# Column blocks for the projections of four fused attention layers on one Trainium2 core

## The chip, the cores and the metric

The kernel runs on one core of one Trainium2 chip, alone. A core has TensorE for matmuls (the profile splits it into PE, the matmuls, and PEld, the loads of their stationary operand), VectorE (DVE), ScalarE (ACT), GpSimd (POOL) and SyncE (SP, here the engine whose queue issues most of the transfers). Matmuls write to PSUM, and VectorE and ScalarE carry their results from there to SBUF. The metric is the device time of one execution in microseconds; the median of some runs is compared.

## The reference, cut to what matters

Four residual layers follow each other on an image batch x of shape (4, 56, 56, 256), all in fp32. Each layer first normalises x over 32 groups of channels (`_gn`).

```
x = x + _L0_conv_ref(_gn(x), ...)   # 7x7 neighbourhood attention, zero padding
x = x + _L1_conv_ref(_gn(x), ...)   # dense graph of 1024 tokens per block
x = x + _L2_conv_ref(_gn(x), ...)   # 7x7 neighbourhood attention, dilation 1 and 2
x = x + _L3_conv_ref(_gn(x), ...)   # 7x7 shifted window attention
return x
```

Layers 0, 2 and 3 share one frame; here it is with the names of layer 2:

```
qkv = (x @ w_qkv + b_qkv).reshape(B, H, W, 3, NUM_HEADS, hd)
...
attn = jnp.einsum('bhijd,bhijkld->bhijkl', q, kg)
attn = attn + rpb[...]
...
attn = jax.nn.softmax(attn.reshape(B, h, H, W, ks * ks), axis=-1)
...
return jnp.einsum('bhijkl,bhijkld->bhijd', attn, vg)
...
return out @ w_proj + b_proj
```

There are 8 heads of 32 channels. A layer thus has four projections of 256 by 256 for each token: queries, keys, values and the output.

## The kernel before

The program's main part is `direct_blocks`; a second, slower form (`fused_blocks`) stands behind a test of the input's range and isn't run here. An image has 3,136 tokens. Channels lie on partitions in two halves (CC = 2), so x is held as 128 partitions by 2 by tokens, and a projection adds up two matmuls, h = 0 and 1, of 128 contracted channels each.

**Projections.** `project` (L941 to L947) makes 128 output channels for 392 tokens (layers 2 and 3, and the output projection of layer 0) or 448 tokens (keys and queries of layer 0): the stationary operand is a 128 by 128 piece of the weight, the normalised tokens stream past it, and the result takes one PSUM bank of tag m, of which there are two (`ps_m`). It is called for keys, queries and the output projection. `value_tiles` (L962 to L980) makes the values the other way round: 128 tokens are stationary and the 256 columns of the weight stream, so that tokens come to lie on partitions; two such tiles share a bank. The last tile of an image has 64 tokens (the 25th). VectorE adds the bias (L975), and the values go to HBM, from where the attention gathers them.

**Attention.** It goes in units. In layers 0 and 2 (`attend_pairs`) a unit is a tile of 7 rows and 12 or 16 columns, for all heads or for four heads of two tiles; in layer 3 (`attend_quads`) it is four heads of eight windows. The logits (L1058, L1012) contract over the 32 channels of one head: four heads are stationary on four blocks of 32 rows of the array at once. VectorE, ScalarE and GpSimd add the masks, take the exponential and multiply by a mask or bias (L1065 to L1069, L1017 to L1019); GpSimd adds two pieces into b (L1078). The products (L1087, L1027) give 32 output channels for each head: four heads write to four blocks of 32 columns, which are the PSUM partitions `j * HD:(j + 1) * HD`. A second set of them, with ones for the values, gives the denominators. VectorE divides (L1237, L1841, L2075, and L1239, L1845, L2077).

**Order.** The work of a unit is written out as logits of this unit, then `fill`, then products of the unit before it:

```
for w in units:
    logits(w)
    if held:
        both(held)
    w["fill"]()
    if held:
        products(held)
        held["done"]()
    held = w
```

`fill` holds the steps of the other work, dealt out over the units by `stream` in each layer: the projections for rows that are needed later (`project_rows`), the values (`values`), the output projection of earlier rows (`project_out`), normalising (`prepare`), and one step of the group statistics (`step_stats`). The statistics have two small matmuls of full width for each layer and image (L912, L921). TensorE so goes from logits in row blocks to projections of the full 128 by 128 array, and from these to products in column blocks, once in nearly every unit. There are 128 units in each of layers 0 and 2 and 64 in layer 3. A scheduler orders layers 0 and 2; layer 3 follows the written order on TensorE, VectorE, ScalarE and GpSimd. Layer 1 uses neither `project` nor `value_tiles`. All four engines wait for each other through semaphores.

The code that the change touches, and what calls it:

Of the kernel before, what the change touches and what calls it, by code (L numbers as in the profile page):

```python
# [34 lines left out]
C = 256  # L35
P = 128
CC = C // P
HD = 32
# [792 lines left out]
def direct_blocks(ctx: ExitStack, tc: tile.TileContext, d: dict, watch):  # L831
# [3 lines left out]
    nc = tc.nc  # L835
# [40 lines left out]
    def ps_m():  # L876
        return psum_tile("m", m_bufs)
# [63 lines left out]
    def project(w, col, rhs, n):  # L941

        pm = ps_m()
        for h in range(CC):
            nc.tensor.matmul(pm[:, :n], lhsT=w[:, h, col:col + P], rhs=rhs(h),  # L945
                             start=(h == 0), stop=(h == CC - 1))
        return pm[:, :n]  # L947

    def evac(i, dst, src):
# [12 lines left out]
    def value_tiles(v, a, c, n, xn, w, bias, dst):  # L962

        t0, t1 = c * n // P, (c + 1) * n // P if (c + 1) * n < T else -(-T // P)
        pm = ps_m()
        sizes = [min(P, T - t * P) for t in range(t0, t1)]
        mine = sizes[2 * a:2 * a + 2]
        for j, k in enumerate(mine):
            first = (2 * a + j) * P
            for h in range(CC):  # L970
                nc.tensor.matmul(pm[:k, j * C:(j + 1) * C], lhsT=xn[:, h, first:first + k], rhs=w[:, h, :],  # L971
                                 start=(h == 0), stop=(h == CC - 1))
        for k in sorted(set(mine)):
            js = [j for j, kj in enumerate(mine) if kj == k]
            nc.vector.tensor_tensor(  # L975
                v[:k, 2 * a + js[0]:2 * a + js[-1] + 1, :], pm[:k, js[0] * C:(js[-1] + 1) * C].rearrange("p (j c) -> p j c", c=C),
                bias[:k].rearrange("p (o c) -> p o c", o=1).to_broadcast([k, len(js), C]), ALU.add)
            t = t0 + 2 * a + js[0]
            nc.sync.dma_start(out=dst[t * P:min((t + len(js)) * P, T), :].rearrange("(k p) c -> p k c", p=k),
                              in_=v[:k, 2 * a + js[0]:2 * a + js[-1] + 1, :])  # L980
# [145 lines left out]
    def layer0(early, big, pool, brief):  # L1126
# [47 lines left out]
        def project_rows(r):  # L1174
# [6 lines left out]
            def values(a):  # L1181
                value_tiles(v, a, g, CH, xn, wv, bv0, vd[b])

            def keys(m):
                pm = project(wk, m * P, lambda h: xn[:, h, at:at + CH], CH)
                rows = pm.rearrange("p (r c) -> p r c", c=S)
                for i in range(NTC):
                    c0, n = key_range(*COLS[i:i + 2])
                    dst = (kE if i in (0, NTC - 1) else kI)[:, m, i // 2, 8 * g:8 * (g + 1), :]
                    nc.scalar.activation(dst, rows[:, :, c0:c0 + n], AF.Identity, bias=bk0[:, m:m + 1])  # L1190

            def queries(m):
                pm = project(wq, m * P, lambda h: xn[:, h, at:at + CH], CH)
                y = 8 * g
                while y < 8 * (g + 1):
                    i, y1 = y // TR, min((y // TR + 1) * TR, 8 * (g + 1))
                    if (b, i) not in q:
                        q[b, i] = brief.tile([P, CC, BT], FP, tag="q", name="q0", bufs=6)
                    nc.scalar.activation(q[b, i][:, m, (y - TR * i) * S:(y1 - TR * i) * S],
                                         pm[:, (y - 8 * g) * S:(y1 - 8 * g) * S],  # L1200
                                         AF.Identity, bias=qbias[:, 0, m:m + 1], scale=SCALE)
                    y = y1
# [53 lines left out]
        def project_out(r):  # L1256
            b, g = divmod(r, NB0)
            x = pool.tile([P, CC, BT], FP, tag="xr", name="xr0")
            nc.sync.dma_start(out=x, in_=tokens_of(0, b, g * BT, BT))

            def step(m):
                pm = project(wo, m * P, lambda h: attns[r][:, h, :], BT)
                nc.vector.scalar_tensor_tensor(x[:, m, :], pm, bo0[:, m:m + 1], x[:, m, :], ALU.add, ALU.add)
                if m:
                    add_stats(1, b, g, x)
                    nc.sync.dma_start(out=tokens_of(1, b, g * BT, BT), in_=x)
            return [lambda m=m: step(m) for m in range(CC)]
# [465 lines left out]
    def layer2(held, big, pool, brief, last_steps):  # L1733
# [27 lines left out]
        def project_rows(i):  # L1761
# [9 lines left out]
            def values(a):  # L1771
                value_tiles(v, a, c, WC2, xn, w_qkv[:, :, 2 * C:], bv2, vd[b])
# [206 lines left out]
    def layer3(early, big, pool, brief):  # L1979
# [69 lines left out]
        def values(r):  # L2049

            b, c = divmod(r, 8)
            xn = xns[r]
            v = pool.tile([P, 4, C], FP, tag="vt", name="vt3", bufs=1)

            def step(a):
                value_tiles(v, a, c, WC, xn, w_qkv[:, :, 2 * C:], bv3, vd[b])
                if a == 0 and r:
                    gather(r - 1)
                if a and r == NIMG * 8 - 1:
                    gather(r)  # L2060
            return [lambda a=a: step(a) for a in range(2)]
# [195 lines left out]
```

## Time and profile before

| | us |
|---|---|
| median of 3 runs | 3989.01 |
| lowest and highest run | 3976.07, 3992.41 |
| span of the profiled execution | 3977.8 |
| TensorE matmul busy | 3814.5 (96%) |
| VectorE busy | 2372.2 (60%) |
| GpSimd busy | 1745.8 (44%) |
| ScalarE busy | 1381.2 (35%) |

The span runs from the first to the last instruction of the profiled execution. Mean granted TensorE clock is 0.983 of full speed. A matmul's end in the trace is modelled and matmuls overlap, so busy time says little of how near TensorE is to its peak; the starts are what counts. An fp32 matmul of the program appears as two matmuls and two weight loads in the trace, called passes below. In a shape such as `128*32 128x392` the first pair is rows and columns of the array in use, the second the partitions and columns of the streamed operand. The lines that carry the argument stand in the prediction.

### The profile page before, as it was taken

How to read it: one execution, taken by the hardware profiler on the slowest of the kernel's cores; microseconds unless marked ns; L12 is line 12 of the kernel's file. 1: busy time of each engine (PE TensorE's matmuls, PEld its weight loads, DVE VectorE, ACT ScalarE, POOL GpSimd, SP SyncE). 2: the span in 40 equal slices, each digit the busy share in tenths (PEclk: the TensorE clock that was granted, in tenths of full speed). 3: DMA queues.
4: the chain of work that ended last, by engine and by line, in shares of the span. 5: the costliest groups of instructions: out<-in, count | busy, mean ns of one | idle time of the engine just before them, and what ended most of it. 6: DMA issues, size and time to landing. Idle time of an engine off the chain costs nothing. (4 is left out here: it accounts for less than half of the span.)

```text
span 3977.8 us, 92350 instructions
## 1 busy us (share of the span) xinstructions
PE 3814.5 (96%) x38871; PEld 2707.4 (68%) x38871; DVE 2372.2 (60%) x4431; ACT 1381.2 (35%) x2927; POOL 1745.8 (44%) x1883
## 2 busy tenths in 40 slices
PE   7999999889999999999999999999999999899998
PEld 4566666557777677776777767776676666566765
DVE  6777777734345544445444553446788887666665
ACT  3455545422222222222222222222555555344443
POOL 3566767721123312233112331123677777555554
PEclk9899999989999999999999999999999999999999
DMA  8343333320000100001000000001344443434442
GB/s 270 104 134 119 113 120 104 99 104 1 24 19 24 40 6 15 20 25 35 6 24 15 25 24 10 10 10 56 111 125 126 125 121 111 157 120 135 127 128 93
DMA packets 268659, 301.84 MB, mean 76 GB/s; under 512 B 25926, under 2 KB 260584, under 8 KB 267752
## 3 DMA queue, kind: packets, MB, share of 16 engines
q1 hardware_dynamic: 267946, 295.76, 23.9%
q8 instruction: 308, 5.05, 0.5%
q14 instruction: 117, 0.96, 0.1%
q10 hardware_dynamic: 288, 0.08, 0.0%
HBM read 203.39 MB, written 92.37 MB: 74 GB/s over the span
## 5 line engine op out<-in xcount | busy, mean ns | idle before, releaser
L1441 DVE TENSOR_TENSOR acc<-acc,ps_v 128x257 f32<-128x257 f32 x1104 | 463.4, 423 | 718.7 <-PE ps_v L1519 690.7
L1519 PE MATMUL ps_v<-xw,e 128*128 128x257 f32 x2208 | 612.6, 382 | 1.2 <-DVE acc L1441 1.2
L1514 PE MATMUL ps_o<-xw,at 128*128 128x257 f32 x2208 | 609.0, 379 | 0.0
L1409 PE MATMUL ps_s<-xnT,xd 128*128 128x512 f32 (+3 forms) x1344 | 572.7, 549 | 3.9 <-DVE xnT L1387 3.9
L1519 PEld LDWEIGHTS ps_v<-xw,e 128*128 128x128 f32 x2208 | 413.5, 189 | 142.7 <-issue 82.4
L1503 ACT COPY at<-ps_t 128x512 f32<-128x512 f32 (+3 forms) x332 | 170.6, 514 | 970.0 <-PE ps_t L1500 969.7
L1078 POOL TENSOR_TENSOR b<-e 126x336 f32<-126x336 f32 (+5 forms) x512 | 500.0, 997 | 9.6 <-ACT e L1066 1.5
L1514 PEld LDWEIGHTS ps_o<-xw,at 128*128 128x128 f32 x2208 | 419.1, 190 | 60.1
L945 PE MATMUL ps_m<-xn,w_wqkv 128*128 128x392 f32 x1024 | 379.1, 504 | 12.3 <-DVE dv L922 3.9
L1402 POOL TENSOR_SCALAR xd<-xnT,vec 128x128 f32<-128x128 f32 x192 | 116.8, 619 | 569.3 <-PE ps_s L1409 565.7
L1069 POOL TENSOR_TENSOR e<-e,m0t 126x672 f32<-126x672 f32 (+3 forms) x128 | 238.6, 1864 | 265.8 <-ACT e L1068 245.4
L1069 POOL TENSOR_TENSOR e<-e,bias 119x784 f32<-119x784 f32 (+5 forms) x128 | 244.0, 1906 | 179.9 <-ACT e L1068 178.6
L1409 PEld LDWEIGHTS ps_s<-xnT,xd 128*128 128x128 f32 x1344 | 225.8, 191 | 141.8 <-issue 126.5
L1412 ACT ACTIVATE e<-ps_s 128x512 f32<-128x512 f32 x336 | 185.4, 552 | 347.8 <-PE ps_s L1409 340.8
L990 ACT ACTIVATE no<-rs 128x168 f32<-128x168 f32 (+2 forms) x256 | 93.8, 367 | 583.8 <-DVE rs L1841 268.3
L945 PEld LDWEIGHTS ps_m<-xn,w_wqkv 128*128 128x128 f32 x1024 | 187.8, 191 | 137.3 <-ACT pr L2097 17.5
L1087 PEld LDWEIGHTS ps_o<-e,vp 124*32 124x32 f32 (+3 forms) x8192 | 177.8, 111 | 147.4 <-issue 97.7
L1087 PE MATMUL ps_o<-e,vp 124*32 124x112 f32 (+3 forms) x8192 | 242.0, 254 | 6.2 <-POOL e L1069 4.4
L1841 DVE RECIPROCAL rs<-ps_o 128x196 f32<-128x196 f32 (+2 forms) x128 | 176.0, 1375 | 87.1 <-PE ps_o L1087 86.6
L939 DVE TENSOR_SCALAR xn<-x,gst 128x28 f32<-128x28 f32 (+4 forms) x368 | 207.5, 616 | 32.3 <-PE ps_m L945 22.9
L1066 ACT ACTIVATE e<-e 126x672 f32<-126x672 f32 (+5 forms) x256 | 219.5, 857 | 20.7 <-DVE e L1065 8.0
L1019 POOL TENSOR_TENSOR e<-e,m3l 98x784 f32<-98x784 f32 x64 | 118.3, 1848 | 217.9 <-ACT e L1016 217.9
(196 smaller groups left out, 6293.8 us busy)
## 6 DMA issues: line engine op xcount, KB each, us to landing
x<-xr SPq DMA_DIRECT2D x64, 392.0 KB
x<-in_x SPq DMA_DIRECT2D x53, 448.0 KB
x<-x SPq DMA_DIRECT2D x60, 392.0 KB
xr<-x SPq DMA_DIRECT2D x60, 392.0 KB
vd<-v SPq DMA_DIRECT2D x72, 256.0 KB
xr<-in_x SPq DMA_DIRECT2D x32, 392.0 KB
xr<-x SPq DMA_DIRECT2D x28, 448.0 KB
x<-xr SPq DMA_DIRECT2D x28, 448.0 KB
```

What stands on the lines that cost most here:

```text
L939: nc.vector.tensor_scalar(dst, src, gst[:, h, 0:1], gst[:, h, 1:2], ALU.subtract, ALU.mult)
L945: nc.tensor.matmul(pm[:, :n], lhsT=w[:, h, col:col + P], rhs=rhs(h), start=(h == 0), stop=(h == CC - 1))
L1066: nc.scalar.activation(ev, ev, AF.Exp)
L1069: nc.gpsimd.tensor_tensor(parts(ev), parts(ev), w["emask"], ALU.mult)
L1078: nc.gpsimd.tensor_tensor(w["b"][a][:nk, :, :2 * nq].rearrange("p h (i c) -> p h i c", i=2), ev[:, :, :, 0, :], ev[:, :, :, 1, :], ALU.add)
L1087: nc.tensor.matmul(w["o"](k, i)[j * HD:(j + 1) * HD], lhsT=ones[:nk, :HD] if k else v(j, u), rhs=w["b"][j // 2][:nk, j % 2, i * nq:(i + 1) ...
L1409: nc.tensor.matmul(s[:, :n], lhsT=xd[j][:, h, :], rhs=xnT[:, h, first * P:last * P], start=(h == 0), stop=(h == CC - 1))
L1412: nc.scalar.activation(e[:, :n], s[:, :n], AF.Exp, scale=5.0)
L1441: nc.vector.tensor_tensor(acc[:, i, :], acc[:, i, :], pv[:, :C + 1], ALU.add)
L1514: nc.tensor.matmul(out[j][:, :C + 1], lhsT=e[:, col(i)] if i == j else at[:, col(i)], rhs=xw[:, i, :], start=(i == j), stop=(i == NB - 1))
L1519: nc.tensor.matmul(pv[:, :C + 1], lhsT=e[:, col(i)], rhs=xw[:, j, :], start=True, stop=True)
L1841: nc.vector.reciprocal(rs.rearrange("p (t c) -> p t c", t=2), pv[:, :, 1, :])
```

## The change

In `project` each of the two matmuls becomes four, and each writes 32 of the 128 partitions of the same bank, from 32 columns of the weight piece, with the same streamed operand. In `value_tiles` the stationary tokens are cut in the same way, k / 32 blocks for a tile of k tokens (four, or two for the last tile of an image). Everything that reads the results is as it was.

```
         pm = ps_m()
         for h in range(CC):
-            nc.tensor.matmul(pm[:, :n], lhsT=w[:, h, col:col + P], rhs=rhs(h),
-                             start=(h == 0), stop=(h == CC - 1))
+            for j in range(4):
+                nc.tensor.matmul(pm[j * HD:(j + 1) * HD, :n], lhsT=w[:, h, col + j * HD:col + (j + 1) * HD], rhs=rhs(h),
+                                 start=(h == 0), stop=(h == CC - 1))
         return pm[:, :n]
...
             for h in range(CC):
-                nc.tensor.matmul(pm[:k, j * C:(j + 1) * C], lhsT=xn[:, h, first:first + k], rhs=w[:, h, :],
-                                 start=(h == 0), stop=(h == CC - 1))
+                for i in range(0, k, HD):
+                    nc.tensor.matmul(pm[i:i + HD, j * C:(j + 1) * C], lhsT=xn[:, h, first + i:first + i + HD], rhs=w[:, h, :],
+                                     start=(h == 0), stop=(h == CC - 1))
```

## The prediction

> **What bounds the kernel now.** I first cut the span into the layers (busy time by window), then asked what TensorE waits for, then read one unit of attention in the timeline. The windows are the start-up, layers 0, 1, 2 and 3; the columns after the length are busy microseconds and instruction counts by engine.
>
> ```profile
> 0.00:88.00 88.00, 60.42 (x546) 38.70 (x550) 56.45 (x121) 29.05 (x72) 24.68 (x27) 0.96 0.83 278
> 88.00:804.00 716.00, 651.57 (x10915) 435.85 (x10908) 541.30 (x764) 340.88 (x794) 476.90 (x378) 0.95 0.38 114
> 804.00:2757.00 1953.00, 1930.67 (x8668) 1419.08 (x8666) 887.41 (x2294) 426.34 (x790) 488.29 (x757) 0.99 0.07 23
> 2757.00:3443.00 686.00, 657.82 (x11435) 457.41 (x11435) 537.52 (x730) 362.25 (x861) 488.61 (x399) 0.99 0.42 125
> 3443.00:3978.00 535.00, 514.00 (x7318) 356.35 (x7318) 349.50 (x526) 222.72 (x411) 267.36 (x322) 0.98 0.39 121
> ```
>
> TensorE is busy 91, 96 and 96% in layers 0, 2 and 3; the next engine, VectorE, has 76, 78 and 65%. The waits of TensorE with a cause are few; these are its largest.
>
> ```profile
> PE ps_m L945 <- DVE attn L1239: 19.0, 10, 3.7
> PE ps_m L912 <- DVE mv L908: 14.2, 1, 14.2
> PE ps_m L945 <- DVE v L975: 11.4, 6, 5.0
> ```
>
> So these layers are bound by TensorE, layer 0 with some slack. But busy is not at its peak, and the timeline shows where time is lost. One unit of layer 3, TensorE alone (start, length, line, tiles, shape):
>
> ```profile
> 3507.98 0.89 PE L1027 MATMUL ps_o<-e,v 98*32 98x98 f32 x32
> 3508.68 0.86 PE L1027 MATMUL ps_o<-e,ones 98*32 98x98 f32 x32
> 3509.47 0.95 PE L1012 MATMUL ps_s<-q,k 32*98 32x98 f32 x32
> 3510.35 1.58 PE L945 MATMUL ps_m<-attn,w_wp 128*128 128x392 f32 x4
> 3511.77 2.80 PE L945 MATMUL ps_m<-xn,w_wqkv 128*128 128x392 f32 x8
> 3514.41 1.03 PE L971 MATMUL ps_m<-w_wqkv,xn 128*128 128x256 f32 x4
> 3515.36 0.89 PE L1027 MATMUL ps_o<-e,v 98*32 98x98 f32 x32
> ```
>
> Starts are to be compared, since ends overlap. The program's fp32 matmul runs as two passes: a projection has two matmuls (h = 0, 1) and shows x4. Eight passes of 392 columns take 3514.41 - 3511.77 = 2.64 us, 0.330 each. The products of 32 columns (98*32) are the form that the change takes: 32 passes of 98 columns in 3508.68 - 3507.98 = 0.70 us, 22 ns each, where one pass alone at 0.330/392 per column would take 82. Four run side by side. The whole unit takes 7.38 us; full streaming would be 16 x 0.082 + 8 x 0.082 + 12 x 0.327 + 4 x 0.213 = 6.74. Most of the 0.64 lies at changes of form.
>
> [...] four L971 passes at 0.216 end at 3514.41 + 0.86 = 3515.27 and the products start at 3515.36, 0.09 us later, though VectorE and GpSimd are long done.[...] where a load is not hidden, after a change of form: from the L945 of 3510.35 to the next are 1.42 us, 0.10 more than four passes at 0.329; the first eight rounds of products take 0.70 us instead of 8 x 0.084, some 0.025 more.[...] the trace shows four at full rate, at 98 columns only.
>
> **The change part by part.**
> Added instructions: the trace has 2,240 passes of L945 and 1,200 of L971. Each becomes four blocks, except 48 passes of the half tile at the end of an image (64 columns), which become two: 3 x 3,392 + 48 = 10,224 passes and as many loads, on TensorE only. The built order on the other engines stays nearly the same: ScalarE and GpSimd are unchanged but for one swap, VectorE and SP move within layer 0's start. No wait is added: the block with j = 0 carries those of the old matmul.
>
> Streaming: four blocks side by side take one old pass. A column costs 0.834 ns (passes of 448 and 256 columns come every 375.7 and 215.6 ns). Rounds of 98 and 84 columns of the products come every 84.9 and 72.6 ns, 3.2 and 2.5 over their columns; the full-width pass has 2.1 over its own. 3,440 rounds x some 0.7 ns = +2.4 us.
>
> Removed, 1: projection to products is no longer a change of form. I counted the passages in the timeline of TensorE: 105 in layer 0, 124 in layer 2, 60 in layer 3 and two at a border, 291 in all. Each loses the drain (0.093) and the exposed first load of the products (0.025): 291 x 0.118 = -34.3 us.
>
> Removed, 2: logits to projection stays a change, from row blocks to column blocks, but the exposed load is 32 columns instead of 128: 0.105 to 0.025. 101 + 115 + 60 + 6 = 282 passages x 0.080 = -22.6 us.
>
> Removed, 3: a load also shows inside the projections when the first pass waited and its load with it: the steps between projection passes that are 25 to 250 ns over the pass sum to 47.8 us; without the 282 x 0.105 above, 18.2. With 0.025 for 0.105, -13.8 us.
>
> Added: the group statistics (L912, L921) and the table look-up stay full width, so a projection next to them now changes form; 11 passages from a projection to L912/L921 at 0.1 to 0.2 and some ten of the table: +3 us.
>
> Sum: -34.3 - 22.6 - 13.8 + 2.4 + 3 = -65 us of TensorE's own time. Not all of it reaches the end. In layers 2 and 3 (43 of the 71 saved) the chain of waits is TensorE's nearly throughout; I let 0.9 through. In layer 0 (28) TensorE still waits some 85 us in stops of over 0.25 us, partly for transfers and weights at the start, so 0.75. 38.5 + 21 - 5.4 = 54, taken as 55. What is late next is GpSimd's b and e (L1078, L1069) and VectorE's evacuation, which already end a few of TensorE's waits in layers 0 and 2.
>
> Unknown costs. Four streams of 392 columns that read the same rows (every block has the same rhs; products read four different slices): the trace bounds it by the products, nothing; the other bound is two at a time, 1,792 x 0.329 + 448 x 0.376 + 1,200 x 0.216 = 1,017 us more. I take nothing, because the tiles run ahead of the order in the program: in one product of layer 2 the third block waits for GpSimd's e, and both passes of the first two blocks run before it, two by two, in the time of two.
>
> ```profile
> 3386.01 0.39 PE L1087 MATMUL ps_o<-e,vp 124*32 124x112 f32 x4
> 3387.13 0.29 PE L1087 MATMUL ps_o<-e,vp 124*32 124x112 f32 x2 [0.74 <-POOL e L1069]
> ```
>
> Four passes one after the other would take 0.10 x 3 up to the last start and then 0.28 for it, 0.57; the row has 0.39.[...] Issue: layer 2 goes from 11,435 to 14,907 passes. The densest 3 us of the trace have 128 passes (23 ns), the densest 50 us 1,081 (46 ns). Layer 2 will need 44 ns on average. Lower bound 0; upper bound below.
>
> **Rivals.**
> A. The drains go, but others take their place (GpSimd at 71% of layer 2, VectorE at 78%): a unit in which the products already wait for b hides nothing more. For it: L1087 waits for L1078 and L1069 today. Against: over the whole trace TensorE waits 9.1 us for b, 4.4 for e and 9.4 for the masked logits (L1065), so these engines are ahead as a rule. If 0 to 30% get through: -20 to 0 us, 3,969 to 3,989 on the median.
> B. Slower: issue of instructions. Place: layers 2 and 3. Price: p ns for each pass with its load. It decides from 660/14,907 = 44 ns in layer 2 and 515/10,790 = 48 in layer 3. At 60 ns, layer 2 takes 894 (+208), layer 3 647 (+112), layer 0 some +80: about 4,390. At 48 ns layer 2 takes 716 (+30) while layers 0 and 3 keep their gain (-35): no change. For it: the dense stretches could come from a queue that filled before. Against: 23 ns over 128 passes.
> C. Slower: the four streams of the same 128 rows hinder each other. Place: each projection. It decides from a round 6.5% longer (66/1,017); at 10% +37 us, 4,026; at two at a time about 4,940. Against: products of 126 rows stream at full rate.
>
> **How the numbers follow.** The profiled execution has a span of 3,977.8 us, 11 below the median of the runs, 3,989.0 (3,976.1 to 3,992.4). 3,989 - 55 = 3,934 is the forecast; its own range, with 30 to 80 us saved, is 3,909 to 3,959, a little wider for the spread of runs: 3,900 to 3,966. Chances: forecast 0.78, A 0.09, B 0.06, C 0.07. The range for 8 in 10 takes in A and the near end of B and C: 3,895 to 4,030. 0.5% is 20 us, about what a measurement of this kernel tells from no change. Faster by more: most of the forecast, 0.77. Within: the rest of it, A, B at 48 ns, 0.11. Slower: 0.12.
>
> **What would show it.** Right: L945 has 8,960 passes, four starting within some 20 ns and the next four 0.33 us later; the step from L971's last round to L1027 is the round alone; the first pass after the logits is 0.025 over the round; the unit above takes about 7.2 us; layer 2 is some 20 us and layer 3 some 12 us shorter. Wrong: rounds of over 0.35 us (C), gaps in TensorE that nothing ended (B), the same gaps now put down to GpSimd or VectorE (A). A clock granted lower than 0.98 would make it wrong in a way that I do not price.

## The result and the profile after

The changed kernel takes 3943.5 us (median of 4 runs, 3941.7 to 3952.9) where the kernel before takes 3982.5 in the same comparison (4 runs, 3975.7 to 3992.4): a ratio of 0.9912, 95% interval 0.9893 to 0.9931, 39 us faster. A second comparison gave 3945.1 against 3984.2 (0.9896, 0.9879 to 0.9914), again 39 us. The forecast was 55.

The profiled execution has a span of 3951.1 us at a mean granted clock of 0.977; that of before had 3977.8 at 0.983. It is the slowest of the four runs; the others were granted 0.980 and 0.981. So the two profiles are only 27 us apart.

Busy time by window, for the start-up and layers 0 to 3 of the changed kernel; columns as in the prediction, PEclk the third from the right.

```profile
0.00:88.00 88.00, 58.05 (x924) 29.35 (x925) 53.45 (x117) 27.74 (x69) 23.05 (x26) 0.92 0.81 272
88.00:796.00 708.00, 635.31 (x13816) 385.46 (x13809) 544.31 (x767) 341.53 (x797) 482.46 (x380) 0.95 0.38 117
796.00:2749.00 1953.00, 1930.75 (x8669) 1421.76 (x8667) 887.44 (x2295) 426.05 (x790) 488.27 (x757) 0.99 0.07 23
2749.00:3424.00 675.00, 646.06 (x14906) 406.81 (x14906) 533.80 (x729) 361.88 (x861) 489.20 (x399) 0.97 0.43 128
3424.00:3951.00 527.00, 504.57 (x10790) 290.11 (x10790) 350.02 (x527) 222.65 (x411) 269.19 (x322) 0.97 0.39 124
```

Layers 0, 2 and 3 are 8, 11 and 8 us shorter, layer 1 is as it was. In layer 2 the clock fell from 0.99 to 0.97; between its first and last logits half-clock steps lost 14 us of full clock, 12 more than before.

The unit of layer 3 in the timeline of TensorE, the same form as the one in the prediction:

```profile
3491.91 0.86 PE L1029 MATMUL ps_o<-e,v 98*32 98x98 f32 x32
3492.59 0.86 PE L1029 MATMUL ps_o<-e,ones 98*32 98x98 f32 x32
3493.38 0.95 PE L1014 MATMUL ps_s<-q,k 32*98 32x98 f32 x32
3494.26 1.52 PE L946 MATMUL ps_m<-attn,w_wp 128*32 128x392 f32 x16
3495.61 2.81 PE L946 MATMUL ps_m<-xn,w_wqkv 128*32 128x392 f32 x32
3498.24 1.05 PE L973 MATMUL ps_m<-w_wqkv,xn 128*32 128x256 f32 x16
3499.10 0.86 PE L1029 MATMUL ps_o<-e,v 98*32 98x98 f32 x32
```

It takes 3499.10 - 3491.91 = 7.19 us, before 7.38. Read the starts again: the record of a pass of 392 columns is 0.49 us long, but the next round starts after 0.329. From the values to the products are 0.86 us, four rounds of 0.216 and nothing else (before 0.95). The 0.09 us that are gone are what the prediction calls the drain: in layer 3 of the kernel before, the products start 0.309 us after the start of the last pass of the values (median of 57 places), here 0.216 us after that of its last round (61 places). The traces show this gap at a change of form, not what TensorE does in it. From the first L946 to the second are 1.35, which is 0.03 over four rounds (before 0.10): the first round after the logits takes 0.354 us (before 0.433; medians of 64 places in layer 3), the others 0.329. That this excess is the load that shows, now shorter, is a reading, from the records of the loads: 0.11 us at 32 columns and 0.19 at 128. Eight rounds of four blocks take 3498.24 - 3495.61 = 2.63 us, 0.329 each, as full-width passes did.

The largest waits of TensorE, by cause (total, times, longest):

```profile
PE ps_m L946 <- DVE attn L1241: 19.9, 10, 3.8
PE ps_m L946 <- DVE v L977: 17.0, 6, 6.2
PE ps_m L912 <- DVE mv L908: 14.3, 1, 14.3
```

They are the same three, and the one for v grew from 11.4 to 17.0 us. One of its stops is at the start: in layer 0 the scheduler sets the order, and it has put VectorE's statistics of late tiles of x ahead of an evacuation. VectorE, then TensorE, in the changed kernel:

```profile
46.07 1.15 DVE L894 BATCH_NORM_STATS2 st<-x 128x6 f32<-128x448 f32 x2 [4.50 <-DMA x<-in_x]
48.08 0.63 DVE L894 BATCH_NORM_STATS2 st<-x 128x6 f32<-128x448 f32 x1 [0.86 <-DMA x<-in_x]
48.62 0.83 DVE L1067 TENSOR_TENSOR e<-ps_s,m0t 90x672 f32<-90x672 f32 x1
49.38 0.61 DVE L894 BATCH_NORM_STATS2 st<-x 128x6 f32<-128x448 f32 x1
49.91 0.40 DVE L977 TENSOR_TENSOR v<-ps_m,bc 128x256 f32<-128x256 f32 x1
```

```profile
50.37 3.21 PE L946 MATMUL ps_m<-xn,w_wk 128*32 128x448 f32 x16 [6.25 <-DVE v L977]
```

The same evacuation and projection in the kernel before:

```profile
46.08 0.41 DVE L975 TENSOR_TENSOR v<-ps_m,bc 128x256 f32<-128x256 f32 x1
46.54 1.77 PE L945 MATMUL ps_m<-xn,w_wk 128*128 128x448 f32 x4 [1.75 <-DVE v L975]
```

The evacuation of 0.40 us stood behind statistics that waited for input until 46 and 48 us, and behind a third at 49 us. In the kernel before it starts at 46.08 us. TensorE stops 6.25 us instead of 1.75, and its next sixteen passes then take 3.21 us instead of 1.77 for the same four rounds, at a granted clock of 0.50. The logits of the third unit start at 55.6 us (before 49.5), those of the ninth at 107.4 (98.0).

### The profile page after: what moved, and what is told of

It is laid out like the page before. It is cut to its first block, busy times and chain, and to the rows that moved or that the text cites. A ratio compares the mean times of both kernels' runs of the same rounds, so it can differ in the third digit from the quotient of the medians.

```text
span 3951.1 us, 112757 instructions
## 1 busy us (share of the span) xinstructions
PE 3774.7 (96%) x49095; PEld 2533.5 (64%) x49095; DVE 2369.0 (60%) x4431; ACT 1379.9 (35%) x2927; POOL 1752.2 (44%) x1883
## 5 line engine op out<-in xcount | busy, mean ns | idle before, releaser
L946 PE MATMUL ps_m<-xn,w_wqkv 128*32 128x392 f32 x4096 | 380.8, 501 | 16.4 <-DVE vt L977 5.2
L1089 PEld LDWEIGHTS ps_o<-e,vp 124*32 124x32 f32 (+3 forms) x8192 | 205.2, 113 | 108.9 <-issue 88.3
L946 PEld LDWEIGHTS ps_m<-xn,w_wqkv 128*32 128x32 f32 x4096 | 124.2, 111 | 196.9 <-issue 130.7
```

Of the source, the lines that this page charges most:

```text
L946: nc.tensor.matmul(pm[j * HD:(j + 1) * HD, :n], lhsT=w[:, h, col + j * HD:col + (j + 1) * HD], rhs=rhs(h), start=(h == 0), stop=(h == CC - 1))
L1089: nc.tensor.matmul(w["o"](k, i)[j * HD:(j + 1) * HD], lhsT=ones[:nk, :HD] if k else v(j, u), rhs=w["b"][j // 2][:nk, j % 2, i * nq:(i + 1) ...
```

## The experiments

Theory: what is paid for is the change of form (the drain, 0.09 us, and the load that shows, 0.10 us at 128 columns and 0.03 at 32), and everything else is as before; what is missing of the 55 us went into the order at the start, into waits for other engines in layer 0, and into the clock (how far that held is said below). The main rivals were that every blocked pass gains by itself, and that blocks of any width would do.

**Two blocks of 64 columns**

```diff
-            for j in range(4):
-                nc.tensor.matmul(pm[j * HD:(j + 1) * HD, :n], lhsT=w[:, h, col + j * HD:col + (j + 1) * HD], rhs=rhs(h),
+            for j in range(2):
+                nc.tensor.matmul(pm[j * 64:(j + 1) * 64, :n], lhsT=w[:, h, col + j * 64:col + (j + 1) * 64], rhs=rhs(h),
...
-                for i in range(0, k, HD):
+                for i in range(0, k, 64):
```

> Every projection of layers 0, 2 and 3 in two blocks of 64 columns side by side instead of four of 32. Theory (the gain is the form: the drain goes only where projection and products have the same width of tile, and the load that shows after the logits shrinks with its columns): projection to products stays a change of form and keeps its 0.093 + 0.025 us; the first load after the logits falls from 0.105 to about 0.053. The unit of layer 3 takes 7.38 - 0.05 = 7.33 us (before 7.38, four blocks 7.19), the step from the last pass round of L973 to L1029 stays near 0.95 us, and the whole is 282 x 0.052 = 15 us faster at most with the loads inside projections 20: some 3965 to 3978 where the kernel before takes 3983. Rival (any column tiles end the drain, whatever their width): the step falls to 0.86 us, the unit takes about 7.22 us, the whole is near the changed kernel, 3945 to 3955. Rival (the gain is finer starts that let loads run beside passes, in proportion to the number of tiles): half the gain, the unit 7.28, the whole about 3963.

Measured: 3969.3 us against 3980.5 before (0.9968, 0.9956 to 0.9981), 11 us faster. One unit of layer 3 in TensorE's timeline:

```profile
3489.04 0.95 PE L1014 MATMUL ps_s<-q,k 32*98 32x98 f32 x32
3489.92 1.54 PE L946 MATMUL ps_m<-attn,w_wp 128*64 128x392 f32 x8
3491.28 2.80 PE L946 MATMUL ps_m<-xn,w_wqkv 128*64 128x392 f32 x16
3493.92 1.03 PE L973 MATMUL ps_m<-w_wqkv,xn 128*64 128x256 f32 x8
3494.88 0.89 PE L1029 MATMUL ps_o<-e,v 98*32 98x98 f32 x32
...
3496.38 0.95 PE L1014 MATMUL ps_s<-q,k 32*98 32x98 f32 x32
```

The unit takes 7.34 us. From the values to the products are again 0.96 us, the drain of before, though both are column tiles: their width differs. The load after the logits shows 0.045 us (1.36 less four rounds), between 0.03 and 0.10. The theory's numbers hold: blocks of 64 columns shorten the load that shows, but keep the drain.

**Only `project` in blocks, and only `value_tiles`**

```diff
# project_only, in value_tiles
-                for i in range(0, k, HD):
-                    nc.tensor.matmul(pm[i:i + HD, j * C:(j + 1) * C], lhsT=xn[:, h, first + i:first + i + HD], rhs=w[:, h, :],
-                                     start=(h == 0), stop=(h == CC - 1))
+                nc.tensor.matmul(pm[:k, j * C:(j + 1) * C], lhsT=xn[:, h, first:first + k], rhs=w[:, h, :],
+                                 start=(h == 0), stop=(h == CC - 1))
# values_only, in project
-            for j in range(4):
-                nc.tensor.matmul(pm[j * HD:(j + 1) * HD, :n], lhsT=w[:, h, col + j * HD:col + (j + 1) * HD], rhs=rhs(h),
-                                 start=(h == 0), stop=(h == CC - 1))
+            nc.tensor.matmul(pm[:, :n], lhsT=w[:, h, col:col + P], rhs=rhs(h),
+                             start=(h == 0), stop=(h == CC - 1))
```

> Only the q, k, out and fused projections (project) in four blocks of 32 columns; the value projections (value_tiles) stay one block of 128. Theory (changes of form are what is paid): after the logits the first load is 32 columns, -0.08 us; from the last projection to the values there is a new change of form, 0.093 + 0.105 = +0.198; from the values to the products nothing changes. The unit of layer 3 takes 7.38 - 0.08 + 0.20 = 7.50 us, so layer 3 is some 7 us longer than before; in layers 0 and 2, where many products follow a q, k or out projection directly, the drain goes at those. On the whole about 20 us faster than before: 3955 to 3970. Rival (each blocked pass gains by itself, by overlap of its load): 65% of the passes are blocked, so 65% of the 39 us: about 3957, and the unit of layer 3 gains 65% of its 0.19 and takes 7.26 us. The unit of layer 3 tells them apart, not the time.

> Only the value projections (value_tiles) in four blocks of 32 columns; q, k, out and fused projections stay one block of 128. Theory (changes of form): in layer 3 a change is added between the last projection and the values (0.093 + 0.025) and one is taken away between the values and the products (the same): the unit takes 7.38 us, as before. In layers 0 and 2 the values often stand between full projections, where two changes are added. The built program has 148 more entries into a form than the kernel before (871 against 686): the sum is 15 to 25 us slower than before, 3997 to 4010. Rival (each blocked pass gains by itself): 35% of 39 us faster, about 3969, and the unit takes 7.31 us.

Measured: project alone 3969.9 us (ratio 0.9973, 0.9963 to 0.9983), 10.5 faster, half of what the theory gave for the whole. Values alone 4000.0 us (1.0045, 1.0028 to 1.0061), 19.5 slower than before, within what it gave; at the clock of the kernel before it would be 10.6 (see the table below), which is under the 15 to 25. The two counts of entries that the expectation names, 871 and 686, differ by 185 and not by 148. The start of layer 0 moved in these kernels and in two_blocks too (the third unit begins at 52.5 to 54.1 us, before at 49.5), so the units are plainer than the totals. Project alone:

```profile
3508.28 0.95 PE L1013 MATMUL ps_s<-q,k 32*98 32x98 f32 x32
3509.16 1.52 PE L946 MATMUL ps_m<-attn,w_wp 128*32 128x392 f32 x16
3510.50 2.82 PE L946 MATMUL ps_m<-xn,w_wqkv 128*32 128x392 f32 x32
3513.25 1.13 PE L972 MATMUL ps_m<-w_wqkv,xn 128*128 128x256 f32 x4
3514.31 0.89 PE L1028 MATMUL ps_o<-e,v 98*32 98x98 f32 x32
...
3515.80 0.95 PE L1013 MATMUL ps_s<-q,k 32*98 32x98 f32 x32
```

Values alone:

```profile
3518.48 0.95 PE L1013 MATMUL ps_s<-q,k 32*98 32x98 f32 x32
3519.36 1.58 PE L945 MATMUL ps_m<-attn,w_wp 128*128 128x392 f32 x4
3520.78 2.80 PE L945 MATMUL ps_m<-xn,w_wqkv 128*128 128x392 f32 x8
3523.51 1.07 PE L972 MATMUL ps_m<-w_wqkv,xn 128*32 128x256 f32 x16
3524.40 0.87 PE L1028 MATMUL ps_o<-e,v 98*32 98x98 f32 x32
...
3525.87 0.34 PE L1013 MATMUL ps_s<-q,k 32*98 32x98 f32 x4
```

With project alone the unit takes 7.52 us, more than before (7.38): the eight rounds up to the values now take 2.75 (drain, 0.12 over their own length) and the values 1.06 (load and drain to the products, 0.20), against 0.08 saved after the logits. With values alone it takes 7.39: 2.73 up to the values, 0.89 from them to the products; the drain has moved one place. Each half of the change by itself gains nothing in this unit: what a shorter load saves after the logits, a new change of form costs again. So blocked passes do not gain each by itself; what counts is what stands beside them. Where products follow `project` directly, as often in layer 2, project alone does gain: layer 2 is 10 us shorter there, from its first logits to its last.

**The blocks one after the other**

```diff
-        for h in range(CC):
-            for j in range(4):
+        for j in range(4):
+            for h in range(CC):
...
-            for h in range(CC):
-                for i in range(0, k, HD):
+            for i in range(0, k, HD):
+                for h in range(CC):
```

> The same four blocks of 32 columns, but issued one block after the other: all passes of block 0, then all of block 1, and so on, instead of the four blocks of each half of the contraction in turn. Nothing else differs. Theory (the tiles take their passes independently and run ahead of the program's order, as the products with a waiting block showed): no change against the changed kernel, 3935 to 3955, the unit of layer 3 takes 7.19 us, the four tiles start side by side. Rival (passes start in the order of the program, one that must wait for its tile holds up those behind it): the four passes of a block take four rounds before the next block starts, a projection takes about 13 rounds instead of 4, the unit of layer 3 goes from 7.19 to some 18 us, and the whole to over 5500. Between the two (a short look-ahead): rounds of 1.2 to 2 times the old ones, the whole 4100 to 5000.

Measured: 3956.4 us (0.9935, 0.9918 to 0.9952), 24 faster than before, nothing like the 5500 of starts in program order. A projection, eight rounds of it, in TensorE's timeline:

```profile
3484.76 2.87 PE L946 MATMUL ps_m<-xn,w_wqkv 128*32 128x392 f32 x32
3487.40 1.12 PE L973 MATMUL ps_m<-w_wqkv,xn 128*32 128x256 f32 x16
```

2.64 us for 32 passes: four tiles side by side, although in the built program all passes of block 0 come before the first of block 1. The weight loads show that TensorE gets them in this order: one load stands ahead of the first pass (3484.44 us) and the others follow from 3484.77 on, where the changed kernel has four loads ahead of its first pass. The first pass of the fourth block stands behind twelve passes of the other three, four of each, and it starts with their first ones; the nine others it overtakes. So a pass that waited for its tile did not hold up those of other tiles here: the projection after the logits takes 1.34 us (3483.42 to 3484.76), four rounds of 0.329 and 0.02, where starts in the order of the program would take the 13 rounds of the rival, 4.3 us by the same 0.329. It isn't quite free: the blocks start 13 ns apart instead of 6 to 7, and the unit takes 7.25 us (3482.55 to 3489.80), 0.06 more than the changed kernel's. At equal clock (table below) it costs about 10 us in all, where the theory said none.

**The start, and layers by themselves**

A flag keeps the full width where it is set, in `project` and in the same way in `value_tiles`:

```diff
+            if full_width[0]:
+                nc.tensor.matmul(pm[:, :n], lhsT=w[:, h, col:col + P], rhs=rhs(h),
+                                 start=(h == 0), stop=(h == CC - 1))
+                continue
...
# start_full, in layer 0's project_rows
+            full_width[0] = r < 5
# layers23: set until layer 2 begins
+        full_width[0] = False
# layer0_only: as start_full, and set again in layer 2
+        full_width[0] = True
```

> The changed kernel, but the projections of the first five rows of layer 0 stay one block of 128 columns; the scheduler then puts VectorE's instructions of the start in the order of the kernel before. Theory (the 10 us that the changed kernel loses up to the ninth unit come from VectorE's statistics of late input standing ahead of a value evacuation, an order that the scheduler chose): the third unit's logits start near 49.5 us as before (changed kernel 55.6), the ninth's near 98 (107.4), L946 no longer waits 6 us for v there, and the whole is 7 to 10 us under the changed kernel: 3932 to 3938 where that takes 3943. Rival (the loss is chance in when the input lands, or is made up later where TensorE waits anyway): the same time as the changed kernel within 3 us. Rival (narrow blocks themselves cost at the start): faster too, but with the order of VectorE the same as in the changed kernel; the order of VectorE in the trace tells.

> Blocks of 32 columns in layers 2 and 3 only; layer 0 stays as before. Theory (layer 0's gain of some 14 us behind its start is nearly eaten by the start, so that layer 0 as a whole gives only 4): the logits of layer 1 begin as before, layers 2 and 3 give their 22 us, the whole is 4 us over the changed kernel, about 3947. Rival (the prediction's own account, layer 0 gives 21 us): some 20 us over the changed kernel, about 3963.

> The changed kernel once more, beside the two others, for the spread of its runs and of its clock: 3943 median, 3938 to 3953, granted clock 0.977 to 0.983. If the clock decides the spread, 0.001 of it goes with 2.5 to 4 us; if not, the times do not follow it.

> Blocks of 32 columns in layer 0 alone, from its sixth row on (so that VectorE's start is that of the kernel before); layers 2 and 3 stay as before. Theory (in layer 0 the other engines take back about half of what TensorE saves: between 160 and 720 us its waits grew from 40 to 47 us): the kernel with the start mended less the one with layers 2 and 3 alone is 15 us at equal clock, so 12 to 16 us faster than before at equal clock. Rival (the prediction's step, three quarters of 28 us come through, and the start was all that ate it): 21 us or more at equal clock. Rival (layer 0 is set by others, its blocks are worth nothing): 0 to 4 us. Both to be read with 2.8 us for each 0.001 of granted clock.

Measured: start_full 3938.4 us (0.9883, 0.9863 to 0.9902), layers23 3957.9 (0.9940, 0.9920 to 0.9959), the changed kernel again 3945.1, all against 3984.2; layer0_only 3962.9 against 3977.2 (0.9965, 0.9953 to 0.9977). The start was the scheduler's order: in start_full VectorE has the order of the kernel before up to 130 us and evacuates at 46 us again, the third unit begins at 49.5 us and the ninth at 98.1, and the stop at the projection shown above is

```profile
46.53 1.77 PE L948 MATMUL ps_m<-xn,w_wk 128*128 128x448 f32 x4 [2.43 <-DVE v L987]
```

The 10 us of the ninth unit were not all kept to the end: the medians are 6.7 us apart, just under the 7 to 10 of the theory, and the runs overlap (3937 to 3942 against 3940 to 3948). For layers23 the theory was wrong: it gave 4 us over the changed kernel, the rival (the prediction's account) 20, and it took 13.

The clock has to be taken out before layers are compared. Over 95 runs of ten kernels, with a level for each kernel, the time falls by 2.8 us (standard error 0.2) for each 0.001 of mean granted clock; in the 39 runs of the kernel before alone the correlation is -0.92. Worked out with this slope:

| kernel | runs | mean clock | less than before, at equal clock, us |
|---|---|---|---|
| before | 39 | 0.9829 | 0 |
| changed | 9 | 0.9799 | 44.6 |
| start_full | 4 | 0.9808 | 48.1 |
| layers23 | 6 | 0.9790 | 33.3 |
| layer0_only | 6 | 0.9842 | 14.1 |
| two_blocks | 7 | 0.9810 | 17.0 |
| project_only | 12 | 0.9830 | 10.5 |
| values_only | 4 | 0.9800 | -10.6 |
| block_by_block | 4 | 0.9795 | 34.4 |

Twice the standard error is 2 to 3 us. The column also takes out what a kernel loses if the change itself lowers the clock. Layers 2 and 3 give 33, layer 0 with the start mended 14, and the sum, 47, is what start_full has (48). The prediction's 21 for layer 0 is out of reach, and so is the rival's 0 to 4. start_full is 3.5 us under the changed kernel, with twice the standard error at 2.8. Waits of TensorE between 160 and 720 us, in the kernel before:

```profile
PE ps_m L945 <- DVE dv L922: 4.4, 3, 2.1
...
PE ps_m L971 <- DVE xr L1263: 3.1, 4, 1.0
```

and in layer0_only:

```profile
PE ps_m L952 <- DVE dv L922: 6.9, 3, 2.3
PE ps_m L983 <- DVE xr L1276: 5.1, 6, 1.5
```

All rows of that view sum to 40.3 us before and to 47.2 here. In layers23, where layer 0 has its old form, they sum to 43.2 and the row for dv is 7.1, so only 4 to 7 us go with the blocks, and the row for dv is not a sign of them. TensorE comes earlier to tiles that VectorE hasn't finished, and stands there for some of what it saved.

**Statistics in blocks too**

```diff
-            nc.tensor.matmul(pm[:, :CC], lhsT=group, rhs=dv, start=True, stop=True)
+            for j in range(4):
+                nc.tensor.matmul(pm[j * HD:(j + 1) * HD, :CC], lhsT=group[:, j * HD:(j + 1) * HD], rhs=dv, start=True, stop=True)
```

(and the same for the mean)

> The changed kernel with the start mended, and the group statistics' matmuls (L912, L921) also in four blocks of 32 columns, so that no change of form is left between them and the projections beside them. Theory: the prediction's price of 3 us for these passages comes back, 2 to 3 us under the kernel with the start mended alone: 3935 to 3937. Rival (these passages stand beside waits of over a microsecond for VectorE, which hide them): the same, 3936 to 3940, or a little more if the order moves.

Measured: 3941.3 us against 3977.2 (0.9906, 0.9891 to 0.9921), at equal clock 48.1 under before, as start_full. That is what the rival gave, not the theory. The order at the start moved again with it, although the first rows have full width as in start_full: the ninth unit begins at 105 us. What the passages themselves are worth stays open; nothing was gained.

## Why the prediction came out as it did

The direction, the mechanism and the range were right; the size was 55 where 39 came. What is missing can be read from TensorE's time between logits, in three parts: work (at full clock), idle stretches of over 0.15 us, and what half-clock steps added to the work. They are worked out from the traces with the modelled ends of the matmuls. Layers 2 and 3 go from their first logits to their last, layer 0 from the first tenth of its logits on, behind the start. In us:

| profile | layer 0: work, idle, half clock | layer 2 | layer 3 |
|---|---|---|---|
| before | 619, 65.5, 26 | 632, 19, 2 | 485, 4, 1 |
| layers23 | 620, 65.8, 22 | 607, 20, 8 | 473, 4, 2 |
| layer0_only | 600, 70.0, 28 | 632, 19, 0 | 485, 4, 0 |
| start_full | 600, 70.1, 28 | 607, 21, 9 | 473, 4, 2 |
| changed | 601, 70.2, 26 | 607, 22, 13 | 473, 4, 2 |

The work repeats within 1 us wherever a layer has the same form. It fell by 19 us in layer 0, 25 in layer 2 and 12 in layer 3.

- **Added: right.** 8,960 passes of L946, four starting within 20 ns and the next four 0.329 us later (medians in layer 3). Rounds kept their length, so rival C falls; no gaps of issue came with 15,000 passes in layer 2, so rival B falls. The argument from 3386.01 us, that tiles run ahead of the order, was right and is now shown by itself (1.34 us for the 16 passes of a projection in block_by_block).
- **Removed, 1 and 2: right.** The step from the values to the products is the rounds alone; the load after the logits shows 0.03 instead of 0.10; the unit takes 7.19 us where "about 7.2" stood. That blocks of 64 columns keep the drain is shown by two blocks (0.96 us to the products), and that both halves are needed in this unit by project and values alone.
- **"Sum: ... -65 us of TensorE's own time": too large, and the first step that failed.** The three layers give 56, and the start of layer 0 can add 2 to 3 (an estimate, a tenth of the 28 forecast for that layer). Terms 1 and 2 alone are 57. So the third term, 13.8 us, less the costs set against it (2.4 for rounds, 3 for statistics and table), comes to 1 or 2 instead of 8. Which of these was mis-sized stays open.
- **"I let 0.9 through" in layers 2 and 3: right.** The work fell by 37 us, where 43 less a share of the costs stood; idle time took back 2, so 0.95 came through. At equal clock layers23 has 33.3. Layer 3, from its first logits to its last, is 10.5 us shorter (foreseen 12), layer 2 11 in the profile at hand and 15 to 17 in four others (foreseen 20).
- **"In layer 0 ... so 0.75": right as a share, but of too much.** Behind the start the work fell by 19 us, where 28 was taken for the whole layer; idle time, most of it for VectorE, took back some 4.5, a quarter. That leaves 14 to 15, and layer0_only has 14.1 at equal clock. Rival A is true to this extent, in this layer.
- **"VectorE and SP move within layer 0's start", costed at nothing: wrong.** It delays the ninth unit by 10 us and costs 3.5 us at the end at equal clock, 6.7 by the medians. I saw the move and did not follow what stood behind it. A priced wait would have been seen: an evacuation behind statistics that wait for transfers, TensorE behind the evacuation.
- **The clock, left unpriced: some 5 to 8 us.** 44.6 at equal clock became 39 in the medians (36 in the means of all runs).

Together: 56 of work, less 7 of idle time, are 49 us at full clock, and start_full has 48 at equal clock. The start takes 3.5 of it and the clock 5.5, which leaves the 39 measured. That the forecast's range held although its sum was too large, its start unpriced and its clock left out owes something to the width of the range.

Where the clock fell can be read at the border of an image in layer 2. From the first statistics (L912) to the second logits after it, before and changed (the clock is the third column from the right):

```profile
3010.00:3023.40 13.40, 10.50 (x160) 7.12 (x156) 10.68 (x14) 5.96 (x13) 8.06 (x8) 1.00 0.53 160
```

```profile
2994.30:3010.20 15.90, 12.28 (x220) 7.26 (x212) 10.97 (x15) 5.95 (x13) 9.88 (x10) 0.82 0.45 138
```

TensorE waits longer for VectorE there (four waits for dv of layer 2 grew from 3.9 to 5.0 us, those for v from 4.7 to 5.5), and then runs at half clock, so that this stretch is 2.5 us longer than before. In the profile of layer0_only, where layer 2 is as before, no half clock falls between its first and last logits. But in values_only, where TensorE's work in layer 2 is not shorter than before, the waits for dv are 5.0 us too and half clock costs 6 us. So longer waits and half clock go together; that it is the faster TensorE which lengthens the waits is not shown. That idle time brings the half clock is the reading of the traces; no run took the idle time away alone.

## What to carry to other kernels

Choose the form of a matmul by its neighbours on TensorE, not by its own cost: here blocks of 32 columns gained because products of 32 columns stood on one side, which saved the drain (0.09 us), and because a narrower load shows less behind the logits on the other (0.03 us instead of 0.10). Half of the change, or another width, kept only about a quarter of the gain by the medians, or made the kernel slower. Count changes of form in the order of execution and price each at the gap and the load that the trace at hand shows. Where a scheduler is between the edit and the program, follow each moved instruction to what it now stands behind; and where a bound engine gets faster, look at the places where it already waits: here a quarter of layer 0's gain turned into waiting, and in layer 2 more half clock came with it.

## What was not expected of the hardware

- Matmuls of one column tile overtook those of others in the order of the program, by nine passes in block_by_block, at 0.06 us for each unit (7.25 us against 7.19).
- A drain was also paid between column tiles of 64 and of 32 columns: 0.09 us in two_blocks (0.96 us from the values to the products, four rounds of 0.216 in it), as between 128 and 32 before (0.95).
- In the clock records of the traces before and after the change the granted clock is 1 or a half, and each stretch of it is a whole number of steps of 3.41 us. Over the eleven profiles, behind the first 60 us, all but at most two of 143 full-clock steps in which TensorE was busy under 0.4 of the time were followed by a half-clock one; about 64 of 81 at 0.4 to 0.5, 47 of 415 at 0.5 to 0.75, 5 of 11,427 above. In the profiles of the kernel before and the changed one alone these are 21 of 21, 13 of 15, 12 of 77 and none of 2,079. A step that was a little under half busy was as a rule followed by half clock here.
